# Attention as a stream of half rows, and delta back in SBUF: one diff with two parts

## The chip, the core and the metric

The kernel runs on one core of a Trainium2 chip. The metric is the device time of one launch in microseconds. A core has five engines that each work through their own instruction queue in order: TensorE (PE) multiplies matrices into PSUM, VectorE (DVE) and ScalarE (ACT) do elementwise work, GpSimd (POOL) does elementwise work too, and SyncE (SP) issues the transfers between HBM and SBUF here. They wait for each other through semaphores.

## What is computed

The input is an image of 256 x 256 positions with 128 channels. Four layers follow each other; each is `x = x + layer(group_norm(x))`, all in float32. Layers 2 and 3 (spectral mixing; a gated recurrence) aren't touched.

Layer 0 is row attention with four heads of 32 channels, with layer norm ahead of it, a bias shared by all rows and a sigmoid gate:

```python
scores = jnp.einsum('bijhd,bikhd->bijkh', q, k) / np.sqrt(C_HIDDEN)
scores = scores + bias[:, None]
a = jax.nn.softmax(scores, axis=-2)
o = jnp.einsum('bijkh,bikhd->bijhd', a, v)
o = (g * o).reshape(b, n, n, HC)
```

Here `g` is `sigmoid(z @ Wg)`, and the result goes through `Wout`. Every one of the 256 rows attends within itself: 256 queries by 256 keys, four times.

Layer 1 is a selective scan. 256 inner channels with 16 states each run over all 65536 positions in four directions:

```python
delta = jax.nn.softplus(dts + dt_bias[None, :, :, None])
dA = jnp.exp(d_t[..., None] * As)
h = dA * h + (d_t * x_t)[..., None] * B_t[:, :, None, :]
y = jnp.einsum('bkdn,bkn->bkd', h, C_t)
```

## The kernel before

`program` runs the layers one after the other. Two stretches of it are touched.

**Attention** is the second half of `layer0` (L144 to L244). 32 blocks of 2048 positions (8 rows) are loaded (L158, L160). For each block there are 16 projections through one PSUM bank `l0b_mm`: four gates (L168, evacuated by ACT with a sigmoid, L169), and four times q (ACT), k (DVE) and v (DVE). Then each row goes through a chain that crosses all engines: eight score products on PE, of which those of the four heads stand on four different groups of 32 rows of the array (L193); bias added on DVE out of PSUM (L201); row maximum on DVE (L205); eight exponentials with row sums on ACT (L208); reciprocal on DVE (L211); scaling on POOL (L212); two times eight transposes on PE into one PSUM tile `l0b_tp`, evacuated once by ACT (L226) and once by DVE (L228); the product with v on PE (L233), heads on four groups of columns; the gate on DVE (L236). Every second row is followed by the output product (L241), the residual sum (L242) and the statistics (L243). The PSUM tiles of scores, transposes, product and `l0b_mm` have one buffer each. The order of the instructions on each engine is settled by a scheduler at build time.

**The scan** is `scan_stream`. Its order is written out by hand (`tc.manual_schedule()`), so that each engine's queue follows the source. The positions come in 512 chunks of 512 (four directions, 128 chunks each), and a chunk has eight groups s = 0 to 7 of four states of one half `dh` of the channels. A group `g` needs:
- the product of B with du, `b_product(g)`, three groups ahead: on POOL for the groups 2, 4 and 6 of a chunk, on DVE for the others (L437)
- four exponentials on ACT into PSUM (L447) and four scans on DVE (L451), by `scans(g)`
- the product of the states with C on POOL, `c_product(g)` (L467), and the sums over states on PE (L486), by `sums`

For the next chunk, delta is prepared meanwhile. PE makes the dt product in a PSUM bank `l1b_mm` of two (L387); ACT makes the tail of the softplus (L401 to L405); `delta(nxt, 0)` and `delta(nxt, 1)` follow the scans of the groups 3 and 4 on DVE. `delta` has two instructions: L412 adds the tail and the positive part and writes the result over the dt product in its PSUM bank, and L413 multiplies that bank with the block of x in SBUF into the PSUM bank `du`. At group 5 ACT copies each of the two banks to SBUF (`delta_copy`, L419), where the exponentials read it, and at group 6 du of the first half for POOL (`du_copy`, L425).

Of the kernel before, what the change touches and what calls it, by code (L numbers as in the profile page):

```python
# [10 lines left out]
F32 = mybir.dt.float32  # L11
AF = mybir.ActivationFunctionType
ALU = mybir.AluOpType
AX = mybir.AxisListType
PSUM = bass.MemoryType.PSUM
# [73 lines left out]
def layer0(c, x, x1, ab, stats):  # L89
# [4 lines left out]
    with ExitStack() as ctx:  # L94
# [46 lines left out]
                nc.sync.dma_start(zs[:, sl], d)  # L141
                nc.sync.dma_start(bs.rearrange("h j k -> h (j k)")[:, sl], bias)

        with ExitStack() as a:  # L144
            one = a.enter_context(tc.tile_pool(name="l0b_one", bufs=1))
            io = a.enter_context(tc.tile_pool(name="l0b_io", bufs=2))
            wk = a.enter_context(tc.tile_pool(name="l0b_wk", bufs=2))
            ps_s = a.enter_context(tc.tile_pool(name="l0b_s", bufs=1, space=PSUM))
            ps_1 = a.enter_context(tc.tile_pool(name="l0b_1", bufs=1, space=PSUM))
            bias = one.tile([P, NH, 2, S], F32, name="l0b_bias")  # L150
            for jt in range(2):
                nc.sync.dma_start(
                    bias[:, :, jt, :], bs[:, bass.ts(jt, P), :].rearrange("h p k -> p h k")
                )
            for b in range(NB):
                sl = bass.ts(b, BL)
                z = io.tile([P, BL], F32, name="l0b_z")
                nc.sync.dma_start(z, zs[:, sl])  # L158
                xt = io.tile([P, BL], F32, name="l0b_x")
                nc.sync.dma_start(xt, x[:, sl])  # L160
                q = wk.tile([P, BL], F32, name="l0b_q")
                k = wk.tile([P, BL], F32, name="l0b_k")
                g = wk.tile([P, BL], F32, name="l0b_g")
                v = wk.tile([P, 16, P], F32, name="l0b_v")
                for j in range(4):
                    cs = bass.ts(j, CH)
                    mm = ps_1.tile([P, CH], F32, name="l0b_mm")
                    nc.tensor.matmul(mm, w["g"], z[:, cs], start=True, stop=True)  # L168
                    nc.scalar.activation(g[:, cs], mm, AF.Sigmoid)  # L169
                for j in range(4):  # L170
                    cs = bass.ts(j, CH)
                    mm = ps_1.tile([P, CH], F32, name="l0b_mm")
                    nc.tensor.matmul(mm, w["q"], z[:, cs], start=True, stop=True)
                    nc.scalar.activation(q[:, cs], mm, AF.Copy, scale=float(1.0 / np.sqrt(32)))
                    mm = ps_1.tile([P, CH], F32, name="l0b_mm")
                    nc.tensor.matmul(mm, w["k"], z[:, cs], start=True, stop=True)
                    nc.vector.tensor_copy(k[:, cs], mm)
                    mm = ps_1.tile([P, 4, P], F32, name="l0b_mm")
                    for i in range(4):
                        nc.tensor.matmul(  # L180
                            mm[:, i], z[:, bass.ts(4 * j + i, P)], w["v"], start=True, stop=True
                        )
                    nc.vector.tensor_copy(v[:, 4 * j : 4 * j + 4], mm)
                for r in range(8):
                    rows = bass.ts(r, S)
                    if r % 2 == 0:
                        gated = wk.tile([P, CH], F32, name="l0b_gated")

                    sc = ps_s.tile([P, NH, 2, S], F32, name="l0b_sc")
                    for jt in range(2):  # L190
                        for h in range(NH):
                            hs = slice(32 * h, 32 * h + 32)
                            nc.tensor.matmul(  # L193
                                sc[:, h, jt],
                                q[hs, bass.ds(r * S + jt * P, P)],
                                k[hs, rows],
                                start=True,
                                stop=True,
                            )
                    e = wk.tile([P, 2 * NH, S], F32, name="l0b_e")  # L200
                    nc.vector.tensor_tensor(  # L201
                        e, sc.rearrange("p h j k -> p (h j) k"), bias.rearrange("p h j k -> p (h j) k"), ALU.add
                    )
                    top = wk.tile([P, 2 * NH], F32, name="l0b_top")
                    nc.vector.tensor_reduce(top, e, AX.X, ALU.max, negate=True)  # L205
                    den = wk.tile([P, 2 * NH], F32, name="l0b_den")
                    for i in range(2 * NH):
                        nc.scalar.activation(  # L208
                            e[:, i], e[:, i], AF.Exp, bias=top[:, i : i + 1], accum_out=den[:, i : i + 1]
                        )  # L210
                    nc.vector.reciprocal(den, den)  # L211
                    nc.gpsimd.tensor_tensor(  # L212
                        e, e, den[:, :, None].to_broadcast([P, 2 * NH, S]), ALU.mult
                    )
                    op = ps_1.tile([P, S], F32, name="l0b_op")
                    at = []
                    for kt in range(2):
                        tp = ps_1.tile([P, NH, 2, P], F32, name="l0b_tp")
                        for h in range(NH):
                            for jt in range(2):  # L220
                                nc.tensor.transpose(  # L221
                                    tp[:, h, jt], e[:, 2 * h + jt, bass.ts(kt, P)], c.ident
                                )
                        ts_ = wk.tile([P, NH, S], F32, name=f"l0b_at{kt}")
                        if kt == 0:
                            nc.scalar.copy(ts_, tp.rearrange("p h j q -> p h (j q)"))  # L226
                        else:
                            nc.vector.tensor_copy(ts_, tp.rearrange("p h j q -> p h (j q)"))  # L228
                        at.append(ts_)
                    for h in range(NH):  # L230
                        hs = slice(32 * h, 32 * h + 32)
                        for kt in range(2):
                            nc.tensor.matmul(  # L233
                                op[hs], v[:, 2 * r + kt, hs], at[kt][:, h], start=kt == 0, stop=kt == 1
                            )
                    nc.vector.tensor_tensor(gated[:, bass.ts(r % 2, S)], op, g[:, rows], ALU.mult)  # L236
                    if r % 2 == 1:
                        j = r // 2
                        cs = bass.ts(j, CH)
                        mm = ps_1.tile([P, CH], F32, name="l0b_mm")  # L240
                        nc.tensor.matmul(mm, w["o"], gated, start=True, stop=True)  # L241
                        nc.vector.tensor_tensor(xt[:, cs], mm, xt[:, cs], ALU.add)  # L242
                        nc.vector.bn_stats(stats[:, 4 * b + j, :], xt[:, cs])  # L243
                nc.sync.dma_start(x1[:, sl], xt)  # L244

# [53 lines left out]
def scan_stream(c, xc2, y, w):  # L301
# [12 lines left out]
    with ExitStack() as a:  # L314
# [18 lines left out]
        def cols(ch):  # L333
            return bass.ds(chunks[ch][1] * CH % BL, CH)
# [70 lines left out]
                nc.scalar.activation(tails[ch, dh], tails[ch, dh], AF.Ln, bias=1.0)  # L405

        def delta(ch, dh):

            if ch >= N:
                return  # L410
            mm = mms[ch, dh]
            nc.vector.scalar_tensor_tensor(mm, mm, 0.0, tails.pop((ch, dh)), ALU.max, ALU.add)  # L412
            nc.vector.tensor_tensor(dus[dh], mm, blocks[ch][0][:, dh, cols(ch)], ALU.mult)  # L413

        def delta_copy(ch, dh):
            if ch >= N:
                return
            dls[ch, dh] = wk.tile([P, CH], F32, name=f"l1b_dl{dh}")
            nc.scalar.copy(dls[ch, dh], mms.pop((ch, dh)))  # L419

        def du_copy(ch):
            if ch >= N:
                return
            dls[ch, "du"] = wk.tile([P, CH], F32, name="l1b_dus")
            nc.scalar.copy(dls[ch, "du"], dus[0])  # L425
# [82 lines left out]
        for dh in range(2):  # L508
            dt(0, dh)
            for part in range(3):  # L510
                softplus(0, dh, part)
            delta(0, dh)
            delta_copy(0, dh)
        du_copy(0)
        for g in range(3):
            b_product(g)
# [1 line left out]
        for ch in range(N):  # L518
            for s in range(NG):
# [15 lines left out]
                if s == 4:  # L535
                    extras = [[lambda: softplus(nxt, 1, 1)], [lambda: softplus(nxt, 1, 2)]]
                if s == 5:
                    extras = [[lambda: delta_copy(nxt, 0)], [lambda: delta_copy(nxt, 1)]]
                if s == 6:
                    extras = [[lambda: du_copy(nxt)], []]  # L540
                if s == 7:
                    extras = [[lambda: xd_copy(ch + 2)], []]
                scans(g, extras)
                if s == 3:
# [558 lines left out]
```

## Time and profile before

| what | value |
|---|---|
| median of 3 runs | 41903.32 us (41897.54 to 41911.51) |
| profiled execution, its own time | 41897.54 us |
| its span, first to last instruction | 41895.7 us |
| TensorE clock granted, mean over the span | 0.847 |
| busy share of the span | PE 74%, DVE 80%, ACT 44%, POOL 69% |
| attention, from its first projection to its end | about 755 to 4932 us |
| scan, from its first dt product to its end | about 7150 to 33700 us |

A group of instructions is named by its line, its engine, its operation, what it writes and reads, and how often it occurs. Behind the bar stand its total busy time in us, the mean duration of one in ns, and the idle time of its engine just ahead of it with the instruction that ended the waiting. Matmuls in float32 are recorded as two passes each. Where several matmuls run at once on parts of the array, the busy time is the time in which any of them ran.

### The profile page before, as it was taken

The page shows a single profiled execution, that of the slowest core. Times are in us where ns is not written, and L with a number is a line of the kernel's source. Part 1 is how long each engine was busy: PE and PEld are TensorE (multiplying, and loading weights), DVE is VectorE, ACT ScalarE, POOL GpSimd, SP SyncE. Part 2 cuts the span into 40 slices and gives each one's busy share as a digit, 9 for nine tenths or more (in the row PEclk, how much of TensorE's full clock was granted, in tenths as well). Part 3 has the DMA queues.
Part 4 walks back from the last instruction along what each step waited for, and adds up shares of the span by engine and source line. Part 5 has one row for each costly group of instructions (what it writes and reads, how often), then busy time and mean ns, then how long its engine had stood idle before and what let it go on. Part 6 is the DMA issues. An engine that isn't in the chain of part 4 may idle for free. (4 is left out here: it accounts for less than half of the span.)

```text
span 41895.7 us, 243807 instructions
## 1 busy us (share of the span) xinstructions
PE 31099.4 (74%) x72752; PEld 12795.4 (31%) x72752; DVE 33637.8 (80%) x27685; ACT 18638.7 (44%) x34732; POOL 28968.4 (69%) x7196
## 2 busy tenths in 40 slices
PE   7676798777777777777777777777777778995555
PEld 1333343222222222222222222222222224542221
DVE  4444301999999999999999999999999954138888
ACT  2333201555555555555555555555555533112222
POOL 1222102999999999999999999999999931004444
PEclk8777899989889989899999999999999988795555
DMA  2000133444444444444555555555555575420000
GB/s 109 25 25 26 36 72 104 184 183 183 184 183 184 185 185 184 184 183 183 190 193 194 194 196 194 194 193 193 195 193 194 195 140 125 124 70 17 16 17 16
DMA packets 2233384, 5911.25 MB, mean 141 GB/s; under 512 B 1149159, under 2 KB 1428408, under 8 KB 1658102
## 3 DMA queue, kind: packets, MB, share of 16 engines
q1 hardware_dynamic: 2232054, 5895.66, 39.7%
q8 instruction: 573, 9.39, 0.1%
q14 instruction: 757, 6.20, 0.0%
HBM read 5236.23 MB, written 659.03 MB: 141 GB/s over the span
## 5 line engine op out<-in xcount | busy, mean ns | idle before, releaser
L486 PE MATMUL l1b_y<-l1b_hc,ident 128*128 128x512 f32 x32768 | 16860.4, 665 | 5393.3 <-POOL l1b_hc L467 5390.0
L451 DVE TENSOR_TENSOR_SCAN l1b_h<-l1b_da,l1b_state,l1b_db 128x512 f32<-128x512 f32 x16384 | 19523.3, 1261 | 47.6 <-ACT l1b_da L447 47.1
L467 POOL TENSOR_TENSOR l1b_hc<-l1b_h,l1b_cc 128x2048 f32<-128x2048 f32 x4096 | 18443.2, 4523 | 1263.0 <-DVE l1b_h L451 1017.8
L447 ACT ACTIVATE l1b_da<-l1b_dl,l_A 128x512 f32<-128x512 f32 x16384 | 11314.4, 691 | 10724.8 <-DVE l1b_h L451 10719.2
L486 PEld LDWEIGHTS l1b_y<-l1b_hc,ident 128*128 128x128 f32 x32768 | 6684.3, 212 | 15598.8 <-POOL l1b_hc L467 7879.0
L437 POOL TENSOR_TENSOR l1b_db<-l1b_bb,l1b_dus 128x2048 f32<-128x2048 f32 x1536 | 6956.1, 4529 | 59.3 <-DMA l1b_bb<-l1b_bc 59.3
L437 DVE TENSOR_TENSOR l1b_db<-l1b_bb,l1b_du 128x2048 f32<-128x2048 f32 x2560 | 5844.3, 2283 | 54.4 <-ACT l1b_dus L425 1.1
L212 POOL TENSOR_TENSOR l0b_e<-l0b_e,l0b_den 128x2048 f32<-128x2048 f32 x256 | 922.1, 3602 | 3246.5 <-DVE l0b_den L211 3244.7
L355 PE MATMUL l1b_mm<-l1b_xc,l_xproj 128*40 128x512 f32 x2048 | 1196.8, 716 | 1386.2 <-ACT l1b_dl L419 525.7
L285 PE MATMUL l1a_mm<-l1a_xp,l1a_taps 128*128 128x512 f32 x4608 | 1992.9, 595 | 168.2 <-DVE l1a_xp L277 168.2
L914 PE MATMUL l_sps<-l_tu,l_phase 14*128 14x256 f32 x1024 | 487.8, 639 | 1673.7 <-DVE l_sp L918 1673.7
L295 POOL COPY l1a_ot<-l1a_o 128x8192 f32<-128x8192 f32 x16 | 226.8, 14175 | 1965.3 <-ACT l1a_o L292 1833.6
L208 ACT ACTIVATE l0b_e<-l0b_e,l0b_top 128x256 f32<-128x256 f32 x2048 | 1013.3, 497 | 941.1 <-DVE l0b_top L205 940.7
L221 PE MATMUL l0b_tp<-ident,l0b_e 128*128 128x128 f32 x4096 | 908.8, 395 | 687.5 <-POOL l0b_e L212 560.3
L270 DVE MEMSET l1a_xp<- 128x68 f32 x8 | 0.9, 115 | 1745.4 <-PE l1a_mm L285 1745.3
L228 DVE COPY l0b_at<-l0b_tp 128x1024 f32<-128x1024 f32 x256 | 313.3, 1224 | 1330.6 <-PE l0b_tp L221 1330.4
L285 PEld LDWEIGHTS l1a_mm<-l1a_xp,l1a_taps 128*128 128x128 f32 x4608 | 875.0, 190 | 1285.4 <-issue 1285.4
L972 POOL TENSOR_TENSOR l_m<-l_q,l_v 128x1024 f32<-128x1024 f32 x256 | 818.1, 3196 | 629.7 <-DVE l_q L966 348.1
L657 POOL TENSOR_TENSOR l1c_y<-l1c_y,l1c_sz 128x512 f32<-128x512 f32 x256 | 347.6, 1382 | 1285.6 <-ACT l1c_y L654 1285.6
L930 PE MATMUL l_gp<-l_wall,l_xn 128*128 128x512 f32 x1024 | 1040.3, 1119 | 224.2 <-DVE l_xn L906 150.0
L924 POOL TENSOR_TENSOR l_mag<-l_amp 128x512 f32<-128x512 f32 x64 | 101.4, 1585 | 1594.8 <-ACT l_amp L922 1521.5
L495 ACT COPY l1b_yo<-l1b_y 128x512 f32<-128x512 f32 x1024 | 595.1, 581 | 1112.7 <-PE l1b_y L486 1112.7
(206 smaller groups left out, 31621.7 us busy)
## 6 DMA issues: line engine op xcount, KB each, us to landing
l1b_bb<-l1b_bc SPq DMA_DIRECT2D x2048, 1024.0 KB
l1b_cc<-l1b_bc SPq DMA_DIRECT2D x2048, 1024.0 KB
l_y<-l1b_yo SPq DMA_DIRECT2D x256, 1024.0 KB
l1b_xc<-l_xc SPq DMA_DIRECT2D x128, 1024.0 KB
l1b_xc<-l_xct SPq DMA_DIRECT2D x128, 1024.0 KB
l1b_yo<-l_y SPq DMA_DIRECT2D x128, 1024.0 KB
l_xc<-l1a_o SPq DMA_DIRECT2D x16, 4096.0 KB
l_xct<-l1a_ot SPq DMA_DIRECT2D x16, 4096.0 KB
```

Of the source, the lines that this page charges most:

```text
L208: nc.scalar.activation(e[:, i], e[:, i], AF.Exp, bias=top[:, i : i + 1], accum_out=den[:, i : i + 1])
L212: nc.gpsimd.tensor_tensor(e, e, den[:, :, None].to_broadcast([P, 2 * NH, S]), ALU.mult)
L221: nc.tensor.transpose(tp[:, h, jt], e[:, 2 * h + jt, bass.ts(kt, P)], c.ident)
L285: nc.tensor.matmul(mm, taps[:, tap, ds_], xp[:, r + dy : r + dy + 2, dx : dx + S], start=tap == 0, stop=tap == 8,)
L355: nc.tensor.matmul(mm[:40], w["xproj"][:, dh, k, :], blocks[ch][0][:, dh, cols(ch)], start=dh == 0, stop=dh == 1,)
L437: eng.tensor_tensor(db, bbs[g // 2], du[:, None, :].to_broadcast([P, G, CH]), ALU.mult)
L447: nc.scalar.activation(da, dls[ch, dh], AF.Exp, scale=w["A"][:, k, dh, n : n + 1])
L451: nc.vector.tensor_tensor_scan(h_, a_, d_, states[k][:, dh, n : n + 1], ALU.mult, ALU.add)
L467: nc.gpsimd.tensor_tensor(hc, hs[g], ccs[g // 2], ALU.mult)
L486: nc.tensor.matmul(ys[j % 2], c.ident, hc[:, i], start=False, stop=j // 2 * G + i == 15)
L930: nc.tensor.matmul(gp, xn[:, bass.ts(i, P)], wall, start=True, stop=False)
L972: nc.gpsimd.tensor_tensor(m2, q, swapped(v), ALU.mult)
```

## The change

The first part moves attention to a function `attention` with an order written out by hand. Its unit is half a row, two heads; there are 512 units. In step u of the stream stand the scores of unit u + 2, the exponentials of u + 1, the transposes of u and the product with v of u - 1, so four units are in flight. The score tile has two PSUM buffers of half the size, the two halves of the transposes have a tile each (`l0b_tp0`, `l0b_tp1`), and `l0b_e` has four buffers. The 16 projections of the next block are spread over the steps 5 to 15 of a block. The sigmoid becomes `0.5 * (1 + tanh(x / 2))`: ACT makes the tanh, the one is added in the gate's instruction, and the half goes into a copy of Wout.

The second part takes the delta of the scan back to SBUF. `delta`'s first instruction writes the SBUF tile `l1b_dl` instead of the PSUM bank, the second reads that tile and x, and `delta_copy` is gone. `du_copy` moves from group 6 to group 5, and `xd_copy` from group 7 to group 6.

```diff
--- before.py
+++ after.py
@@ -141,107 +141,177 @@
                 nc.sync.dma_start(zs[:, sl], d)
                 nc.sync.dma_start(bs.rearrange("h j k -> h (j k)")[:, sl], bias)
...
-            ps_s = a.enter_context(tc.tile_pool(name="l0b_s", bufs=1, space=PSUM))
-            ps_1 = a.enter_context(tc.tile_pool(name="l0b_1", bufs=1, space=PSUM))
...
+        attention(c, x, x1, zs, bs, w, stats)
+def attention(c, x, x1, zs, bs, w, stats):
+    tc, nc = c.tc, c.nc
+    BL, NH = 2048, 4
+    NB = NPOS // BL
+    UB = 16
+    N = UB * NB
+    with ExitStack() as a:
+        one = a.enter_context(tc.tile_pool(name="l0b_one", bufs=1))
+        io = a.enter_context(tc.tile_pool(name="l0b_io", bufs=2))
+        wk = a.enter_context(tc.tile_pool(name="l0b_wk", bufs=2))
+        ps2 = a.enter_context(tc.tile_pool(name="l0b_p2", bufs=2, space=PSUM))
+        ps1 = a.enter_context(tc.tile_pool(name="l0b_p1", bufs=1, space=PSUM))
+        bias = one.tile([P, NH, 2, S], F32, name="l0b_bias")
+        wo = one.tile([P, P], F32, name="l0b_wo")
+        nc.vector.tensor_scalar(wo, w["o"], 0.5, None, ALU.mult)
+        for jt in range(2):
+            nc.sync.dma_start(
+                bias[:, :, jt, :], bs[:, bass.ts(jt, P), :].rearrange("h p k -> p h k")
+            )
+        blocks, es, tops, dens, ats, ops, gates = ({} for _ in range(7))
+        def load_block(b):
+            k = blocks[b] = {}
+            for n, src in (("z", zs), ("x", x)):
+                k[n] = io.tile([P, BL], F32, name=f"l0b_{n}")
+                nc.sync.dma_start(k[n], src[:, bass.ts(b, BL)])
+            for n in "qkg":
+                k[n] = wk.tile([P, BL], F32, name=f"l0b_{n}")
+            k["v"] = wk.tile([P, 16, P], F32, name="l0b_v")
+        def project(b, i):
+            k = blocks[b]
+            j, n = i // 4, "kqvg"[i % 4]
+            cs = bass.ts(j, CH)
+            mm = ps1.tile([P, CH], F32, name="l0b_mm")
+            if n == "v":
+                for m in range(4):
+                    nc.tensor.matmul(
+                        mm[:, bass.ts(m, P)], k["z"][:, bass.ts(4 * j + m, P)], w["v"], start=True, stop=True
+                    )
+                nc.vector.tensor_copy(k["v"][:, 4 * j : 4 * j + 4].rearrange("p m o -> p (m o)"), mm)
+                return
+            nc.tensor.matmul(mm, w[n], k["z"][:, cs], start=True, stop=True)
+            if n == "k":
+                nc.vector.tensor_copy(k["k"][:, cs], mm)
+            elif n == "q":
+                nc.scalar.activation(k["q"][:, cs], mm, AF.Copy, scale=float(1.0 / np.sqrt(32)))
+            else:
+                nc.scalar.activation(k["g"][:, cs], mm, AF.Tanh, scale=0.5)
+        def scores(u):
+            k, r, hp = blocks[u // UB], u % UB // 2, u % 2
+            sc = ps2.tile([P, 2, 2, S], F32, name="l0b_sc")
             for jt in range(2):
...
+                for h in range(2):
+                    hs = slice(32 * (2 * hp + h), 32 * (2 * hp + h) + 32)
+                    nc.tensor.matmul(
+                        sc[:, h, jt],
+                        k["q"][hs, bass.ds(r * S + jt * P, P)],
+                        k["k"][hs, bass.ts(r, S)],
+                        start=True,
+                        stop=True,
+                    )
+            e = es[u] = wk.tile([P, 4, S], F32, name="l0b_e", bufs=4)
+            nc.vector.tensor_tensor(
+                e,
+                sc.rearrange("p h j k -> p (h j) k"),
+                bias[:, 2 * hp : 2 * hp + 2].rearrange("p h j k -> p (h j) k"),
+                ALU.add,
+            )
+            top = tops[u] = wk.tile([P, 4], F32, name="l0b_top")
+            nc.vector.tensor_reduce(top, e, AX.X, ALU.max, negate=True)
+        def exps(u):
+            e, top = es[u], tops.pop(u)
+            den = wk.tile([P, 4], F32, name="l0b_den")
+            for i in range(4):
+                nc.scalar.activation(
+                    e[:, i], e[:, i], AF.Exp, bias=top[:, i : i + 1], accum_out=den[:, i : i + 1]
                 )
-            for b in range(NB):
...
-                    nc.scalar.activation(g[:, cs], mm, AF.Sigmoid)
...
-                    sc = ps_s.tile([P, NH, 2, S], F32, name="l0b_sc")
+            nc.vector.reciprocal(den, den)
+            nc.gpsimd.tensor_tensor(e, e, den[:, :, None].to_broadcast([P, 4, S]), ALU.mult)
+        def transposes(u):
+            e = es.pop(u)
+            for kt in range(2):
+                tp = ps1.tile([P, 2, 2, P], F32, name=f"l0b_tp{kt}")
+                for h in range(2):
                     for jt in range(2):
...
+                        nc.tensor.transpose(tp[:, h, jt], e[:, 2 * h + jt, bass.ts(kt, P)], c.ident)
+                at = ats[u, kt] = wk.tile([P, 2, S], F32, name=f"l0b_at{kt}")
+                if kt == 0:
+                    nc.scalar.copy(at, tp.rearrange("p h j q -> p h (j q)"))
+                else:
+                    nc.vector.tensor_copy(at, tp.rearrange("p h j q -> p h (j q)"))
+        def product(u):
+            k, r, hp = blocks[u // UB], u % UB // 2, u % 2
+            if hp == 0:
+                ops[u // 2] = ps1.tile([P, S], F32, name="l0b_op")
+            for h in range(2):
+                hs = slice(32 * (2 * hp + h), 32 * (2 * hp + h) + 32)
+                for kt in range(2):
+                    nc.tensor.matmul(
+                        ops[u // 2][hs],
+                        k["v"][:, 2 * r + kt, hs],
+                        ats[u, kt][:, h],
+                        start=kt == 0,
+                        stop=kt == 1,
                     )
...
-                        tp = ps_1.tile([P, NH, 2, P], F32, name="l0b_tp")
...
+            for kt in range(2):
+                del ats[u, kt]
+        def gate(row):
+            b, r = divmod(row, 8)
+            if r % 2 == 0:
+                gates[row // 2] = wk.tile([P, CH], F32, name="l0b_gated")
+            nc.vector.scalar_tensor_tensor(
+                gates[row // 2][:, bass.ts(r % 2, S)],
+                blocks[b]["g"][:, bass.ts(r, S)],
+                1.0,
+                ops.pop(row),
+                ALU.add,
+                ALU.mult,
+            )
+        def out(pair):
+            b, j = divmod(pair, 4)
+            xt, cs = blocks[b]["x"], bass.ts(j, CH)
+            mm = ps1.tile([P, CH], F32, name="l0b_mm")
+            nc.tensor.matmul(mm, wo, gates.pop(pair), start=True, stop=True)
+            nc.vector.tensor_tensor(xt[:, cs], mm, xt[:, cs], ALU.add)
+            nc.vector.bn_stats(stats[:, pair, :], xt[:, cs])
+            if j == 3:
+                nc.sync.dma_start(x1[:, bass.ts(b, BL)], xt)
+                del blocks[b]
+        a.enter_context(tc.manual_schedule())
+        load_block(0)
+        for i in range(UB):
+            project(0, i)
+        scores(0)
+        scores(1)
+        exps(0)
+        for u in range(N + 3):
+            b, i = divmod(u, UB)
+            if u >= 3 and u % 2 == 1:
+                gate((u - 3) // 2)
+            if i == 4 and b + 1 < NB:
+                load_block(b + 1)
+            if u + 2 < N:
+                scores(u + 2)
+            if u + 1 < N:
+                exps(u + 1)
+            if u < N:
+                transposes(u)
+            if 5 <= i and b + 1 < NB:
+                project(b + 1, i - 5)
+            if 1 <= u <= N:
+                product(u - 1)
+            if u >= 5 and (u - 5) % 4 == 0:
+                out((u - 5) // 4)
+            if 5 <= i < 10 and b + 1 < NB:
+                project(b + 1, i + 6)
@@ -405,18 +475,13 @@
                 nc.scalar.activation(tails[ch, dh], tails[ch, dh], AF.Ln, bias=1.0)
         def delta(ch, dh):
-
             if ch >= N:
                 return
-            mm = mms[ch, dh]
-            nc.vector.scalar_tensor_tensor(mm, mm, 0.0, tails.pop((ch, dh)), ALU.max, ALU.add)
-            nc.vector.tensor_tensor(dus[dh], mm, blocks[ch][0][:, dh, cols(ch)], ALU.mult)
-
-        def delta_copy(ch, dh):
-            if ch >= N:
-                return
-            dls[ch, dh] = wk.tile([P, CH], F32, name=f"l1b_dl{dh}")
-            nc.scalar.copy(dls[ch, dh], mms.pop((ch, dh)))
+            dl = dls[ch, dh] = wk.tile([P, CH], F32, name=f"l1b_dl{dh}")
+            nc.vector.scalar_tensor_tensor(
+                dl, mms.pop((ch, dh)), 0.0, tails.pop((ch, dh)), ALU.max, ALU.add
+            )
+            nc.vector.tensor_tensor(dus[dh], dl, blocks[ch][0][:, dh, cols(ch)], ALU.mult)
         def du_copy(ch):
             if ch >= N:
@@ -510,7 +575,6 @@
             for part in range(3):
                 softplus(0, dh, part)
             delta(0, dh)
-            delta_copy(0, dh)
         du_copy(0)
         for g in range(3):
             b_product(g)
@@ -535,10 +599,8 @@
                 if s == 4:
                     extras = [[lambda: softplus(nxt, 1, 1)], [lambda: softplus(nxt, 1, 2)]]
                 if s == 5:
-                    extras = [[lambda: delta_copy(nxt, 0)], [lambda: delta_copy(nxt, 1)]]
+                    extras = [[lambda: du_copy(nxt)], []]
                 if s == 6:
-                    extras = [[lambda: du_copy(nxt)], []]
-                if s == 7:
                     extras = [[lambda: xd_copy(ch + 2)], []]
                 scans(g, extras)
                 if s == 3:
```

More of the change, by code (lines that the diff above doesn't have):

```diff
@@ L142, in layer0 @@
                 nc.sync.dma_start(bs.rearrange("h j k -> h (j k)")[:, sl], bias)
[L144 to L147, printed above, removed]
-            ps_s = a.enter_context(tc.tile_pool(name="l0b_s", bufs=1, space=PSUM))
-            ps_1 = a.enter_context(tc.tile_pool(name="l0b_1", bufs=1, space=PSUM))
-            bias = one.tile([P, NH, 2, S], F32, name="l0b_bias")
-            for jt in range(2):
-                nc.sync.dma_start(
-                    bias[:, :, jt, :], bs[:, bass.ts(jt, P), :].rearrange("h p k -> p h k")
-                )
-            for b in range(NB):
[L156 to L168, printed above, removed]
-                    nc.scalar.activation(g[:, cs], mm, AF.Sigmoid)
[L170 to L187, printed above, removed]
-                    sc = ps_s.tile([P, NH, 2, S], F32, name="l0b_sc")
-                    for jt in range(2):
[L191 to L202, printed above, removed]
-                    )
[L204 to L217, printed above, removed]
-                        tp = ps_1.tile([P, NH, 2, P], F32, name="l0b_tp")
[L219 to L244, printed above, removed]
```

## The prediction

> **What bounds the kernel now.** First the busy time by stage, from windows over the middle of attention and of the scan (us; the clock is TensorE's granted share):
>
> ```profile
> core 0: us, PE busy (x) PEld busy (x) DVE busy (x) ACT busy (x) POOL busy (x), PEclk, DMA share, GB/s
> 800.00:4800.00 4000.00, 2800.03 (x13812) 1473.54 (x13810) 1840.33 (x1726) 1470.95 (x4508) 893.27 (x248) 0.76 0.07 24
> ...
> 8000.00:33000.00 25000.00, 18673.36 (x36678) 7196.79 (x36676) 24871.64 (x19791) 13858.67 (x25101) 23817.74 (x5311) 0.91 0.50 189
> ```
>
> In attention no engine is full (PE 70%, DVE 46%): a chain bounds it. 755 to 4932 us is 4,177 us, or 16.3 us a row. In the scan DVE is full (99.5%) and POOL nearly so (95%), so whatever DVE gains or loses there moves the end. The view of waits in attention shows the chain:
>
> ```profile
> POOL l0b_e L212 <- DVE l0b_den L211: 3146.9, 217, 56.9
> DVE l0b_at L228 <- PE l0b_tp L221: 1288.1, 227, 7.4
> ACT l0b_e L208 <- DVE l0b_top L205: 910.7, 217, 6.3
> ACT l0b_at L226 <- PE l0b_tp L221: 760.6, 248, 6.9
> ```
>
> Every engine waits for the step ahead of it: scores, sum, maximum, exponentials, scaling, transposes, product, one row after the other. Third the groups by shape in which the second part of the change works, and one that shows what may happen to it:
>
> ```profile
> L451 DVE TENSOR_TENSOR_SCAN l1b_h<-l1b_da,l1b_state,l1b_db 128x512 f32<-128x512 f32 x16384 | 19523.3, 1261 | 47.6 <-ACT l1b_da L447 47.1 <-POOL l1b_hc L467 0.2
> L413 DVE TENSOR_TENSOR l1b_du<-l1b_mm,l1b_xc 128x512 f32<-128x512 f32 x1024 | 715.8, 699 | 35.1
> L971 DVE TENSOR_TENSOR l_m<-l_p,l_v 128x1024 f32<-128x1024 f32 x256 | 686.5, 2681 | 0.0
> L983 DVE TENSOR_TENSOR l_p<-l_p,l_qq 128x1024 f32<-128x1024 f32 x192 | 232.5, 1211 | 1.2 <-POOL l_qq L979 1.2
> ```
>
> L971 and L983 (layer 3) are one operation of one shape, both inputs in SBUF, and differ by 1.47 us. The timeline of layer 3 tells why (start, duration):
>
> ```profile
> 38028.80 2.27 DVE L984 TENSOR_TENSOR l_q<-l_q,l_tr 128x1024 f32<-128x1024 f32 x1 [1.15 <-POOL l_tr L978]
> 38030.99 3.36 DVE L971 TENSOR_TENSOR l_m<-l_p,l_v 128x1024 f32<-128x1024 f32 x1
> ...
> 38028.73 1.26 POOL L979 TENSOR_TENSOR l_qq<-l_q 128x512 f32<-128x512 f32 x1
> 38029.95 3.32 POOL L972 TENSOR_TENSOR l_m<-l_q,l_v 128x1024 f32<-128x1024 f32 x1
> ```
>
> L984 starts while L979 runs and ends 1.08 us after it; L971 likewise ends 1.08 us after L972 (33.27). A DVE instruction with two SBUF inputs stands until the running POOL instruction is done, and the POOL instruction behind waits for DVE (3.32 us instead of 2.33).
>
> Last the same view in the scan: L413, today with one input in PSUM, starts in the midst of POOL work and isn't held (0.70 us):
>
> ```profile
> 20042.71 0.70 DVE L413 TENSOR_TENSOR l1b_du<-l1b_mm,l1b_xc 128x512 f32<-128x512 f32 x1
> ...
> 20050.94 0.70 DVE L413 TENSOR_TENSOR l1b_du<-l1b_mm,l1b_xc 128x512 f32<-128x512 f32 x1
> ...
> 20014.13 4.51 POOL L467 TENSOR_TENSOR l1b_hc<-l1b_h,l1b_cc 128x2048 f32<-128x2048 f32 x1 [2.34 <-DVE l1b_h L451]
> 20018.60 4.52 POOL L437 TENSOR_TENSOR l1b_db<-l1b_bb,l1b_dus 128x2048 f32<-128x2048 f32 x1
> ...
> 20036.52 9.00 POOL L467 TENSOR_TENSOR l1b_hc<-l1b_h,l1b_cc 128x2048 f32<-128x2048 f32 x2
> 20045.49 4.52 POOL L437 TENSOR_TENSOR l1b_db<-l1b_bb,l1b_dus 128x2048 f32<-128x2048 f32 x1
> ```
>
> **What the Trainium skill says.** "SBUF — State Buffer", section "Who interferes with whom": a VectorE instruction with two SBUF inputs contends with a GpSimd instruction that reads SBUF, as its second input comes through a shared read interface; whoever starts first keeps it for the whole instruction. Layer 3 agrees, to the 1.08 us above. "ScalarE: Activation LUTs", section "Table sets: the hidden batching unit": exp and tanh are in one set. The trace of before agrees on the other half: sigmoid and exp in turn cost 64 table loads of 1.283 us; a tanh is in no run yet. "TensorE: Matmul & The Clock Gate", section "What's actually happening": the default clock is throttled, and activity releases it. It is 0.76 in attention with its gaps and 0.97 in the convolution (5000 to 7100 us, PE 93% busy), so a denser stream should be near 1.
>
> **Part one, attention, per unit of half a row.** PE: the timeline has 12 score passes of four heads in 1.13 us though one lasts 0.37 to 0.48, so four heads run abreast. With two heads the eight passes of a unit still take four turns, about 1.05 us for half a row; the product the same, 1.0. Eight transposes at 0.11 (full clock) and a switch: 1.05. One projection per unit on average, two passes at 0.533: 1.07; a quarter of an output product: 0.27. Sum 4.44 at full clock, 8.9 a row; splitting the heads costs PE about 2 us a row.
> DVE: sum 1.26 and maximum 1.10 (halves of L201's 2.29 and L205's 2.26, plus their fixed part), reciprocal 0.12, copy 0.61, half a gate 0.17, half of k or v 0.31, a quarter of residual and statistics 0.33: 3.9. ACT: four exponentials 2.0, copy 0.5, half a projection 0.3: 2.8, without table loads. POOL 1.83 (half of 3.60). None of these three binds.
> The chain between units: reciprocal u + 1 stands on DVE behind sum and maximum of u + 2. From the end of the scores of u + 2: 1.26 + 1.10 + 0.19 + 1.83 and four hand-overs of about 0.1 are 4.75 us until the transposes of u + 1, which stand one step on. So a step is at least about 4.6 to 4.75. PE's sum is near that, so neither hides the other: a projection must also be evacuated (0.6) before the one bank is free for the output product. I add 0.5 for these meetings: 5.2 us. Bounds: 4.8 (chain alone) and 5.8 (PE at clock 0.8). 512 x 5.2 = 2,660, with 40 us for 16 projections ahead of the first unit and the drain: 2,700. **Saving 4,177 - 2,700 = 1,480 us** (1,170 to 1,680). Loads of blocks: issued some ten units before use, landing in some 4 us: hidden, otherwise 4 us for each of 31 blocks.
>
> **Part two, the scan, per chunk.** Delta's first instruction still has one SBUF input (dt product in PSUM): 0.67, no change. The second now reads `l1b_dl` and x, both in SBUF: 0.68 alone, but it has to wait for POOL.
> Where POOL is at that moment: each chunk it catches up with DVE and waits for the scans of group 6 (2.34 us at 20014.13). From there seven instructions run back to back at 4.48 us: C6, B2, C7, C0, B4, C1, C2, till 20045.5. Their inputs are ready (nearest: C0, by some 2 us), and these scans don't shift when DVE stands later. The first du comes up at 20042.71, **2.8 us too early**. It then runs 0.6, POOL's B6 having waited; B6 and C3 take 8.96 from there, and the second du comes up after 2.20 + 4.72 + 0.71 = 7.63: **1.3 us too early**. DVE stands 4.14 us a chunk; what is late next is everything behind on DVE, the full engine: product, scans, and POOL's C. POOL has 2.4 us of slack and gets 4.1 more; ACT and PE wait for DVE already. 511 x 4.14 = **2,116 us**, minus 0.02 x 1024 = 20.
> Bounds: 3.0 (each du finds POOL a little later in its instruction) to 5.5 us (POOL keeps the lag of today: 2.8 + 3.6 less what it gains), 1,530 to 2,810.
> The rest costs nothing here: the two ACT copies (L419, 0.577 each, 590 us in all) are gone, from an engine busy 55% which waits 10,103 us for DVE's scans; freeing the PSUM banks earlier lets the x projection and the sums behind it run earlier on PE, hidden under DVE; `du_copy` and `xd_copy` one group earlier are again ACT under DVE, and the transfer of B and C that `xd_copy` starts leaves SP's queue no later.
>
> **Sum**, on the profiled execution, span 41,895.7: - 1,480 + 2,116 - 20 = + 616, so 42,512; the median lies 7.6 above that span, so **42,520 us**, +1.5%.
>
> **Rivals.**
> - No lasting hold in the scan, attention as above: 41,903 - 1,480 = 40,420. It would take POOL instructions that let DVE in between; or the waits shrink as POOL's idle time grows and du falls into it. The point is 1,480 / 511 = 2.9 us a chunk; less, and the kernel is faster. For it: L971's wait is seen behind POOL instructions of 2.3 us, not of 4.5. Against: each full wait in layer 3 ends with the POOL instruction. Chance 0.11.
> - The two nearly cancel (2.7 to 3.1 us a chunk, or attention at 4.1 us a unit): 41,900, chance 0.04.
> - PE becomes attention's bound: at half clock a pass takes twice, and a unit about 8 us; at 5.8 to 7 us the saving is 1,170 to 550 and the time 42,830 to 43,450. For it: layer 3 stays at clock 0.56 with PE 60% busy. Against: no gap over 1 us is left for PE. Chance 0.08.
> - POOL's next instruction gets in ahead of the waiting DVE: 4.48 more per du, 1,022 x 4.48 = 4,580, so 47,100. Against: L984 got in ahead of L972. Chance 0.03.
> - The likeliest, part two outweighs part one: 42,520, chance 0.74; its own range 42,100 to 42,950.
>
> **The numbers.** A measurement of this kernel tells about 0.2% (84 us) from no change. Faster 0.11, within 0.04, slower 0.85. The ends of both parts give 41,903 + 1,530 - 1,680 = 41,750 and 41,903 + 2,810 - 1,170 = 43,540; both at once are unlikely, so 41,850 to 43,150 leaves out about 0.2.
>
> **What would show it.** L413's successor at about 2.7 us mean with two sorts (3.4 and 2.0), L467 and L437 on POOL longer by 0.6 us where they follow it; chunks of 55.8 us instead of 51.7; no idle time on DVE, as the hold counts as busy. Attention of 2,700 us, PE 85% busy at a clock over 0.9, no table loads. Wrong if du stays near 0.7 us, or attention takes over 3,000.

## The result and the profile after

| | before | after |
|---|---|---|
| median | 41907.42 us (4 runs) | 42573.69 us (4 runs, 42511.01 to 42643.39) |
| ratio | | 1.0159, 95% interval 1.0142 to 1.0177 |
| span of the profiled execution | 41895.7 us | 42561.5 us |
| attention, first projection to last statistics | 4,168 us | 2,738 us |
| scan, first x projection to last copy of y | 26,547 us | 28,639 us |

The forecast was 42,520. Attention gives 1,430 us, the scan takes 2,092, and 2,092 - 1,430 = 662 is the difference of the spans (665.8) but for some 3 us.

The windows over attention and scan, as before (us; the clock is TensorE's):

```profile
core 0: us, PE busy (x) PEld busy (x) DVE busy (x) ACT busy (x) POOL busy (x), PEclk, DMA share, GB/s
800.00:3400.00 2600.00, 2248.18 (x13790) 1253.48 (x13792) 1928.68 (x2709) 1426.39 (x4687) 931.53 (x493) 0.95 0.10 37
...
8000.00:33000.00 25000.00, 18269.23 (x34009) 7049.30 (x34008) 24870.73 (x18346) 12493.48 (x22367) 22470.57 (x4922) 0.87 0.46 175
```

In attention PE is busy 86% at a clock of 0.95, after 70% at 0.76. In the scan DVE counts as busy for 99.5% as before, yet the same 25,000 us hold 18,346 DVE instructions where they held 19,791. A busy share doesn't show this loss; the count per window does. The groups by shape show where it is:

```profile
L516 DVE TENSOR_TENSOR_SCAN l1b_h<-l1b_da,l1b_state,l1b_db 128x512 f32<-128x512 f32 x16384 | 19528.8, 1260 | 60.0 <-ACT l1b_da L512 56.9
L484 DVE TENSOR_TENSOR l1b_du<-l1b_dl,l1b_xc 128x512 f32<-128x512 f32 x1024 | 2792.7, 2727 | 35.3
L481 DVE SCALAR_TENSOR_TENSOR l1b_dl<-l1b_mm,l1b_tail 128x512 f32<-128x512 f32 x1024 | 676.7, 661 | 10.0 <-issue 9.7 <-ACT l1b_tail L475 0.3
```

The scans and delta's first instruction cost what they did. The second one, du, went from 715.8 to 2,792.7 us: +2,077, nearly the whole loss. The timeline of one chunk (start, duration):

```profile
20029.23 3.35 DVE L484 TENSOR_TENSOR l1b_du<-l1b_dl,l1b_xc 128x512 f32<-128x512 f32 x1
...
20040.11 1.87 DVE L484 TENSOR_TENSOR l1b_du<-l1b_dl,l1b_xc 128x512 f32<-128x512 f32 x1
...
20023.04 8.99 POOL L532 TENSOR_TENSOR l1b_hc<-l1b_h,l1b_cc 128x2048 f32<-128x2048 f32 x2
20031.99 4.98 POOL L502 TENSOR_TENSOR l1b_db<-l1b_bb,l1b_dus 128x2048 f32<-128x2048 f32 x1
20036.93 9.44 POOL L532 TENSOR_TENSOR l1b_hc<-l1b_h,l1b_cc 128x2048 f32<-128x2048 f32 x2
```

The first du starts at 20029.23, in POOL's two products with C that end at 20032.03, and is done 0.55 us after them; POOL's next product takes 4.98 us instead of 4.52, as it has du ahead of it. The second du starts at 20040.11 and is done 0.55 us after the product with C that began at 20036.93 and ended near 20041.4. It is so throughout: each of the 1,022 du inside the stream ends 0.55 to 0.57 us after the end of a POOL instruction.

The waits in attention, 800 to 3400 us (total, times, longest), answer to the four of before (800 to 4800 us there, most of the stage in both):

```profile
POOL l0b_e L232 <- DVE l0b_den L231: 1418.1, 395, 63.1
ACT l0b_at L243 <- PE l0b_tp L240: 463.9, 399, 3.1
...
DVE l0b_e L215 <- PE l0b_sc L207: 357.0, 279, 4.2
...
DVE l0b_at L245 <- PE l0b_tp L240: 18.1, 35, 1.6
```

DVE's wait for the transposes is down from 1,288 us to 18, ACT's from 761 to 464, and DVE now waits for scores, which stand in PE's queue behind other work: the chain of one row has become a chain of four units that PE nearly fills.

### The profile page after: what moved, and what is told of

Same layout as the page of the kernel before. It is cut to its first block, busy times and chain, and to the rows that moved or that the text cites. A ratio compares the mean times of both kernels' runs of the same rounds, so it can differ in the third digit from the quotient of the medians.

```text
span 42561.5 us, 246934 instructions
## 1 busy us (share of the span) xinstructions
PE 31613.5 (74%) x72752; PEld 12997.0 (31%) x72752; DVE 35804.3 (84%) x28710; ACT 18192.7 (43%) x33901; POOL 29466.7 (69%) x7452
## 5 line engine op out<-in xcount | busy, mean ns | idle before, releaser
L551 PE MATMUL l1b_y<-l1b_hc,ident 128*128 128x512 f32 x32768 | 17991.5, 703 | 6886.9 <-POOL l1b_hc L532 6882.1
L532 POOL TENSOR_TENSOR l1b_hc<-l1b_h,l1b_cc 128x2048 f32<-128x2048 f32 x4096 | 18663.5, 4573 | 2904.8 <-DVE l1b_h L516 2904.8
L551 PEld LDWEIGHTS l1b_y<-l1b_hc,ident 128*128 128x128 f32 x32768 | 7114.6, 226 | 17762.8 <-POOL l1b_hc L532 9357.7
L502 POOL TENSOR_TENSOR l1b_db<-l1b_bb,l1b_dus 128x2048 f32<-128x2048 f32 x1536 | 7183.0, 4676 | 59.7 <-DMA l1b_bb<-l1b_bc 59.7
L484 DVE TENSOR_TENSOR l1b_du<-l1b_dl,l1b_xc 128x512 f32<-128x512 f32 x1024 | 2792.7, 2727 | 35.3
L232 POOL TENSOR_TENSOR l0b_e<-l0b_e,l0b_den 128x1024 f32<-128x1024 f32 x512 | 968.9, 1892 | 1774.6 <-DVE l0b_den L231 1467.1
L490 ACT COPY l1b_dus<-l1b_du 128x512 f32<-128x512 f32 x512 | 299.7, 585 | 2057.4 <-DVE l1b_db L502 2057.4
```

The source lines that it names most:

```text
L232: nc.gpsimd.tensor_tensor(e, e, den[:, :, None].to_broadcast([P, 4, S]), ALU.mult)
L484: nc.vector.tensor_tensor(dus[dh], dl, blocks[ch][0][:, dh, cols(ch)], ALU.mult)
L502: eng.tensor_tensor(db, bbs[g // 2], du[:, None, :].to_broadcast([P, G, CH]), ALU.mult)
L532: nc.gpsimd.tensor_tensor(hc, hs[g], ccs[g // 2], ALU.mult)
L551: nc.tensor.matmul(ys[j % 2], c.ident, hc[:, i], start=False, stop=j // 2 * G + i == 15)
```

## Experiments

The theory: DVE stands in each du until POOL's running instruction is done, because both inputs are in SBUF; how long follows from where POOL is at that moment. Rivals: the loss comes from what else the second part moves (the copies on ACT, `du_copy`, `xd_copy`, delta written to SBUF by DVE), or du with two SBUF inputs has a fixed price. For attention: the chain with PE bounds it, or PE alone.

### Each part alone

`e1_attention_alone` has the new attention and the scan of before; `e2_scan_alone` the reverse.

> The new attention with the old scan. If the two parts add, attention keeps the 1,429 us that the traces show (4,167 to 2,738) and the scan stays at 26,540 us: 41,905 - 1,430 = 40,475 us. If the stages share something (SBUF layout, the end of one overlapping the start of the next), the time lies off this by more than 100 us.

> The old attention with the new scan. If the parts add: 41,905 + 2,092 = 44,000 us, and the mean of the du instruction is again about 2.7 us. If the loss in the scan depended on the new attention ahead of it, it would shrink: under 43,700 us.

Measured: 40,491.34 us (ratio 0.9658, 0.9644 to 0.9673) and 44,021.45 us (1.0503, 1.0485 to 1.0520). The parts add: - 3.42% and + 5.03% make + 1.61%, and both together have + 1.59%. The stage lengths are close to those of the changed kernel (attention 2,745 after 2,738 there, scan 28,589 after 28,639), and the mean of du in `e2_scan_alone` is 2.67 us. So the loss in the scan doesn't depend on the attention ahead of it.

### du with one SBUF input, everything else as changed

```diff
             dl = dls[ch, dh] = wk.tile([P, CH], F32, name=f"l1b_dl{dh}")
-            nc.vector.scalar_tensor_tensor(
-                dl, mms.pop((ch, dh)), 0.0, tails.pop((ch, dh)), ALU.max, ALU.add
-            )
-            nc.vector.tensor_tensor(dus[dh], dl, blocks[ch][0][:, dh, cols(ch)], ALU.mult)
+            mm, tail = mms.pop((ch, dh)), tails.pop((ch, dh))
+            nc.vector.scalar_tensor_tensor(dl, mm, 0.0, tail, ALU.max, ALU.add)
+            nc.vector.scalar_tensor_tensor(mm, mm, 0.0, tail, ALU.max, ALU.add)
+            nc.vector.tensor_tensor(dus[dh], mm, blocks[ch][0][:, dh, cols(ch)], ALU.mult)
```

> As the changed kernel, but delta is made twice on DVE: once into SBUF for the exponentials, once in place in the PSUM bank from which du is made. So the copies on ACT stay away and all else stays moved as in the change, but du has one SBUF input. If the two SBUF inputs are the cause, du is back at 0.70 us, a chunk takes 51.7 + 2 x 0.71 = 53.1 us, and the time is 41,905 - 1,430 + 511 x 1.4 = 41,200 us. If the missing copies, the earlier du_copy and xd_copy, or delta written by DVE into SBUF are the cause, the loss stays and the second delta comes on top: about 43,300 us.

Measured: 41,051.56 us (0.9793, 0.9776 to 0.9809). Its du, by shape:

```profile
L484 DVE TENSOR_TENSOR l1b_du<-l1b_mm,l1b_xc 128x512 f32<-128x512 f32 x1024 | 716.8, 700 | 35.3
```

du is at 0.70 us again, in all 1,024 cases. DVE does one instruction more per half and the kernel is 1,520 us faster than the changed one. The scan takes 27,111 us, 564 over before, or 0.55 us for each extra instruction: less than the 0.71 I had put. In the trace the instruction behind the extra one, which doesn't read its result, starts 0.58 us after it. The result speaks against the copies, the moved steps and delta's way to SBUF as causes: they are all still as in the change. What makes the difference is the place of one operand.

### du moved in DVE's queue

Three kernels move delta and du in DVE's queue. In `e4_first_du_later` the first, in `e5_both_du_later` both stand behind the next product of B on DVE:

```diff
                 b_product(g + 3)
+                if s == 4:
+                    delta(nxt, 0)
+                if s == 5:
+                    delta(nxt, 1)
                 extras = [[], []]
...
-                if s == 3:
-                    delta(nxt, 0)
-                if s == 4:
-                    delta(nxt, 1)
```

> As the changed kernel, but each delta with its du stands behind the next product of B on DVE (2.2 us later in the queue), nothing else. If DVE stands until the POOL instruction in flight ends, the first du waits about 0.5 us instead of 2.7 and the second 1.3 as before, a chunk takes 53.3 us, and the time falls by 511 x 2.2 = 1,120 us to about 41,450 us. If two SBUF inputs merely make du slow (a fixed price of some 2 us each), nothing changes: 42,570 us.

> As the changed kernel, but only the first delta with its du stands behind the next product of B on DVE; the second stays. By POOL's phase the first du waits about 0.5 us instead of 2.7, but POOL's next two instructions then start at the same time as before while DVE comes to the second du 2.2 us sooner, so that this one waits 3.5 us instead of 1.3: a chunk takes 55.5 us and the time stays at 42,570 us within 100. If each du had a waiting time of its own, the first gain would be kept: 41,450 us.

Measured: 42,085.47 us for both (1.0036, 1.0023 to 1.0049) and 43,676.00 us for the first alone (1.0429, 1.0413 to 1.0444). The direction of the first holds, but of the 1,120 us expected it gives only 488; the second is a miss by 1,100 us. The trace of `e5_both_du_later` shows the part that I had left out:

```profile
20050.58 5.03 DVE L484 TENSOR_TENSOR l1b_du<-l1b_dl,l1b_xc 128x512 f32<-128x512 f32 x1
...
20161.89 1.05 DVE L484 TENSOR_TENSOR l1b_du<-l1b_dl,l1b_xc 128x512 f32<-128x512 f32 x1
```

```profile
20050.55 4.50 POOL L502 TENSOR_TENSOR l1b_db<-l1b_bb,l1b_dus 128x2048 f32<-128x2048 f32 x1
...
20153.38 9.01 POOL L532 TENSOR_TENSOR l1b_hc<-l1b_h,l1b_cc 128x2048 f32<-128x2048 f32 x2
```

At 20161.89 du comes up 0.5 us ahead of the end of POOL's products and takes 1.05, about as expected. At 20050.58 it comes 0.03 us after POOL has begun the next one, and stands for all of it. In the changed kernel's trace nearly all first du take 2.7 to 3.4 us: the two engines' phase spreads by some 0.7 us. Moving du by 2.2 puts its arrival within 0.5 us of the border, so part of the cases fall over it: counted over the trace, 138 of 511 first du took 4.6 us or more, at a cost of 651 us over the usual 1.05, which is the miss (635). They are of two kinds. 116 stood for one POOL instruction too many (460 us): they came up after it had begun, or at most 0.11 us ahead of the end of the one before, and then the next one still went first. The other 22 took 9.4 to 10.0 us (192 us): here too POOL's next instructions went ahead of du, 16 times although du had come up 0.12 to 0.53 us before the border (more of this below). The usual chunk takes 53.4 us in the median, and 53.3 was expected. In `e4_first_du_later` it is 227 of 511 (1,036 us), 32 of them waits of 9.2 to 10.0 us. The second du there takes 4.1 us where it doesn't, so that its waiting did grow to the 3.5 expected: what the first saved came back at the second, and the border came on top.

So a third kernel keeps away from the border. `e9_du_three_scans_earlier` puts each delta behind the first scan of its group. Its input has to be ready sooner, so the softplus on ACT moves forward with it (not in this excerpt):

```diff
                 nc.vector.tensor_tensor_scan(
                     h_, a_, d_, states[k][:, dh, n : n + 1], ALU.mult, ALU.add
                 )
+                if i == 0 and then:
+                    then()
...
-                scans(g, extras)
+                then = None
+                if s in (3, 4):
+                    then = lambda: delta(nxt, s - 3)
+                scans(g, extras, then)
```

> As the changed kernel, but each delta with its du stands behind the first scan of its group instead of the fourth (3.5 us earlier in DVE's queue; the softplus on ACT one group earlier accordingly). By POOL's phase the first du then comes up 1.7 us ahead of the end of a product with C, with over a microsecond to either side, and the second 1.3 as before: a chunk takes 54.5 us instead of 55.4, and the time falls by some 480 us to 42,090. If in addition POOL's next instruction only gets ahead of a waiting du where products with B and with C take turns, as in the runs so far, none of the long waits of 11 to 12 us occurs, which is worth another 190 us: 41,900. If du had a fixed price, 42,570 us.

Measured: 42,014.28 us (1.0023, 1.0014 to 1.0031), between the two numbers. Scans and du, by shape:

```profile
L516 DVE TENSOR_TENSOR_SCAN l1b_h<-l1b_da,l1b_state,l1b_db 128x512 f32<-128x512 f32 x16384 | 19689.0, 1263 | 154.9 <-ACT l1b_da L512 145.8 <-issue 0.7 <-POOL l1b_hc L534 0.4
...
L484 DVE TENSOR_TENSOR l1b_du<-l1b_dl,l1b_xc 128x512 f32<-128x512 f32 x1024 | 1918.6, 1874 | 34.8
```

In the median the first du takes 2.04 us and the second 1.75, and a chunk 54.73 instead of 55.5. The 0.2 us over the expected 54.5 are mostly the scans' waits for their exponentials (146 us in all, 57 in the changed kernel), as the softplus is now dense on ACT. A fixed price of du is out: the same instruction on the same operands took 1.05, 2.04, 3.35 or 5.03 us by its place in the queue. One long wait (10.98) was left.

### Attention: which order bounds it

`e6_reciprocal_first` puts the reciprocal of unit u + 1 ahead of the maximum of u + 2 on DVE; `e7_reciprocal_project` moves the projection ahead of the transposes on PE too. Both have the scan of before.

```diff
             if u + 1 < N:
                 exps(u + 1)
+            if u + 2 < N:
+                maxima(u + 2)
+            if 5 <= i and b + 1 < NB:
+                project(b + 1, i - 5)
             if u < N:
                 transposes(u)
-            if 5 <= i and b + 1 < NB:
-                project(b + 1, i - 5)
```

`maxima` is the two lines of the row maximum, taken out of `scores`; `e6_reciprocal_first` has only the first added pair.

> The new attention with the old scan, and on DVE the reciprocal of unit u + 1 stands ahead of the row maximum of u + 2 instead of behind it. If the chain from the scores over DVE and POOL to the transposes bounds attention together with PE, a unit falls from 5.27 to about 5.0 us and the time is some 100 us under that of the new attention with the old scan, about 40,370 us. If PE alone is the bound, the time stays at 40,475 us.

> As the kernel with the reciprocal first, and on PE the projection for the next block stands ahead of the transposes instead of behind them, so that PE has work while POOL scales. If both waits of PE count, a unit falls to about 4.85 us, and the time is some 200 us under that of the new attention with the old scan: about 40,270 us. If PE is full, nothing is gained by the order of its work: 40,475 us.

Measured: 40,216.34 us (0.9602, 0.9586 to 0.9618) and 40,130.36 us (0.9581, 0.9567 to 0.9595). Attention takes 2,499 and 2,409 us after 2,745, so a unit (less 40 us at the ends) is 4.80 and 4.63 us after 5.28: both gains are larger than expected. PE's waits for the scaled exponentials between 900 and 3100 us, of the new attention alone, then of the two:

```profile
PEld l0b_tp L240 <- POOL l0b_e L232: 299.5, 261, 2.3
PE l0b_tp L240 <- POOL l0b_e L232: 202.1, 157, 1.9
```

```profile
PEld l0b_tp L242 <- POOL l0b_e L234: 120.2, 170, 1.2
PE l0b_tp L242 <- POOL l0b_e L234: 54.9, 119, 0.8
```

```profile
PEld l0b_tp L242 <- POOL l0b_e L234: 86.4, 119, 1.2
PE l0b_tp L242 <- POOL l0b_e L234: 43.5, 89, 0.8
```

The windows from 900 to 3100 us, of the three in the same order:

```profile
core 0: us, PE busy (x) PEld busy (x) DVE busy (x) ACT busy (x) POOL busy (x), PEclk, DMA share, GB/s
900.00:3100.00 2200.00, 1904.90 (x11664) 1059.06 (x11664) 1631.90 (x2293) 1206.73 (x3966) 790.00 (x418) 0.95 0.10 38
900.00:3100.00 2200.00, 1997.78 (x12796) 1133.23 (x12792) 1770.54 (x2515) 1303.70 (x4343) 864.17 (x458) 0.99 0.11 42
900.00:3100.00 2200.00, 2066.62 (x13309) 1193.07 (x13309) 1841.17 (x2615) 1360.62 (x4520) 899.14 (x476) 1.00 0.12 43
```

The chain over the reciprocal was a bound beside PE. With it shortened PE's clock also rose from 0.95 to 0.99 and 1.00, which I hadn't counted; how much of the gain is the shorter wait and how much the clock was not measured apart. `e7_reciprocal_project` is the fastest kernel of the study, 4.2% under before; PE is busy 94% in its attention.

### The gate by sigmoid

`e8_sigmoid_gate` evacuates the gate with a sigmoid in the places of the tanh (`AF.Sigmoid`, no one added, Wout not halved), with the scan of before.

> The new attention with the old scan, but the gate by sigmoid, evacuated in the places where the tanh is. Each of the 128 gates then needs two table loads of 1.283 us between exponentials, 328 us on ACT. If ACT's idle 45% hides them, the time stays at 40,475 us. If they delay the exponentials that the next step needs, up to 330 us are lost: 40,600 to 40,800 us; I expect about 40,650.

Measured: 40,575.04 us (0.9686, 0.9672 to 0.9701), against 0.9658 (0.9644 to 0.9673) with the tanh: the intervals just touch. The stage lengths of the traces are plainer. The table loads inside attention:

```profile
L199 ACT ACT_TABLE_LOAD x125 | 160.4, 1283 | 2.3
L228 ACT ACT_TABLE_LOAD x125 | 160.4, 1283 | 2.2
```

321 us of loads, and attention is 76 us longer (2,821 after 2,745): so three quarters of the loads fall into time in which ACT was idle. The tanh is worth these 76 us within the stream, not the 321 of the loads it avoids, and less than the 175 I expected. How the rest of attention's 1,430 us divides between the order, the second score buffer and the split transposes was not measured.

## Why the prediction was right

**The hold in the scan** happened as read from layer 3, and the one operand is its cause (`e3_two_deltas`). Mean of du: 2.73 us, forecast 2.7; the two sorts 3.35 and 1.89 in the median, forecast 3.4 and 2.0; the median chunk 55.5 and the mean 55.9, forecast 55.8; the scan + 2,092, forecast 2,096.

**Two errors cancel in that sum,** so that it meets to 4 us is luck. The waits of usual chunks were over-sized: without the long ones the first du takes 3.21 us in the mean (2.5 of waiting, not 2.8, as the phase spreads downwards from the one chunk I read), the second 1.89 (1.2, not 1.3): 3.7 a chunk instead of 4.14, or 230 us less. And the rival "POOL's next instruction gets in ahead of the waiting DVE", to which I gave a chance of 0.03 for the whole scan, happened in 16 of 511 chunks of the trace. One of them:

```profile
13761.70 12.29 DVE L484 TENSOR_TENSOR l1b_du<-l1b_dl,l1b_xc 128x512 f32<-128x512 f32 x1
...
13764.46 4.52 POOL L502 TENSOR_TENSOR l1b_db<-l1b_bb,l1b_dus 128x2048 f32<-128x2048 f32 x1
13768.92 4.51 POOL L532 TENSOR_TENSOR l1b_hc<-l1b_h,l1b_cc 128x2048 f32<-128x2048 f32 x1
13781.42 4.49 POOL L532 TENSOR_TENSOR l1b_hc<-l1b_h,l1b_cc 128x2048 f32<-128x2048 f32 x1 [7.99 <-DVE l1b_h L516]
```

du starts at 13761.70; the product that runs then ends at 13764.5, but the next two go first, and du is done only when POOL itself has to wait for DVE's scans. It is so in all 16. Each such case costs about 9 us at the first du and 2.8 at the second, 16 of them 188 us. The step "the POOL instruction behind waits for DVE", which I took from two cases in layer 3, is therefore a rule with exceptions.

**Attention**: 2,738 us, forecast 2,700; saving 1,430, forecast 1,480. PE busy 86% at 0.95 (forecast 85%, over 0.9), and 2 table loads in place of 65. Eight score passes of two heads take 1.13 us in the timeline (forecast 1.05), as twelve of four heads did, so for the scores the price of splitting the heads is there; no kernel with all four heads abreast in the stream was tried. The chain was put together too short: its maximum is set at 1.10 us, less than half of L205's 2.26, and takes 1.22 (L222), and the scaling takes 1.89, not 1.83. With these the same sum is some 4.9 us, not 4.75 (an estimate, with the four hand-overs as forecast). The 0.5 us a unit that I added "for these meetings" had no row behind it; that the unit came out at 5.27 against 5.2 is in part luck. What it stands for is shown by `e6_reciprocal_first` and `e7_reciprocal_project`: waits for the scaled exponentials are a part of it, and two moves in the order make a unit 0.65 us shorter, with a clock that rises to 1.

**The steps costed at nothing** were close to nothing. In `e3_two_deltas` they are all as in the change; its scan is 564 us longer than before, and 1,024 extra instructions at 0.58 us would make 596, so all the rest together is worth less than 50 us. The sum of the two parts, each measured alone, agrees with both together within 0.02% of the time. The loads of blocks stay hidden: no wait for them appears among the long ones of attention.

## What to carry to other kernels

Before an operand goes from PSUM to SBUF, count the SBUF inputs of every VectorE instruction that reads it and look up what GpSimd does at that moment: here one such instruction took 0.7 to 12 us, while its engine counted as busy and the busy share stayed at 99.5%. The price is a phase between two queues, so it can be worked out from a timeline, but the place must lie away from a border by more than the spread of the phase, or the result is a mixture. In a stream written by hand, look for what a short instruction stands behind: a reciprocal of 0.2 us behind a maximum of 1.2 cost attention 9%, the lower clock that came with it included.

## What the runs showed of the hardware

A GpSimd instruction that is queued can go ahead of a VectorE instruction that already waits. Long waits of this kind were seen in 16 of 511 first du of the changed kernel (14 of them in its first 256 chunks), in 11 of 511 in `e2_scan_alone` (10), in 32 in `e4_first_du_later` (26) and in 22 in `e5_both_du_later` (19). In all of these the instruction that ended and the one that followed were of different lines: a product with C and one with B, or the reverse. Where a product with C followed one with C there was one such case in some 2,550 (in `e9_du_three_scans_earlier`). A change of line isn't enough, though: the second du of that kernel waits 509 times between a product with B and one with C, and none of these waits was long. Why these chunks and not their neighbours, which in most cases have a phase within 0.1 us of theirs, stays open.

The border between "waits for this instruction" and "waits for the next one too" lies a little ahead of the end: in `e4_first_du_later` and `e5_both_du_later` 76 first du came up at most 0.12 us before the end of a product with C and stood for the following product with B as well. The shortest lead with which du was done behind the running product alone is 0.10 us.
